# A transformer layer on one core: block tails ahead of leftovers, other places for group loads, maxima sent by ScalarE, scaling on GpSimd, and the readback of the sums one step later

## The chip, the cores and the metric

The kernel runs on one core of a Trainium2 chip. The time is the device time of one execution in microseconds. The core has five engines, each with an instruction queue of its own that it works off in order: TensorE (PE; matrix products, with PEld for the loading of the stationary operand), VectorE (DVE), ScalarE (ACT), GpSimd (POOL) and SyncE (SP). SP computes nothing; in this kernel it starts nearly all transfers between device memory and the core. A transfer waits on its issuing queue until what it reads is there and the buffer that it fills is free, and whatever stands behind it in that queue waits as well.

## The reference, cut to what matters

The input x is 16 batches of 512 rows by 512 columns, all in fp32. Each batch goes through attention and a gated feed-forward part:

```
n = layernorm(x)
q, k, v = n Wq + bq, n Wk + bk, n Wv + bv      # 32 heads of 16 columns
q, k = rope(q), rope(k)                        # y * cos + (halves swapped) * sin
out = softmax(causal(q k / 4)) v
x1 = x + layernorm(out Wo + bo)
h = silu((layernorm(x1) Wg) * gs) * ((layernorm(x1) Wu) * us)   # 1408 columns
x2 = x1 + layernorm((h Wd) * ds)
```

Wg, Wu and Wd hold only -1, 0 and 1 in the given data.

## The kernel before, in words

**Number format.** TensorE has a reduced fp32 format here (`fp32r`). Where an operand must stay exact it is cut into a high and a low part (`yh`, `yl`; `hh`, `hl`), and two products are summed. If the feed-forward weights survive the rounding to `fp32r` unchanged, they need only one part. The kernel tests this at run time: `check_weights` (L197) makes 22 checks, each a cast on ScalarE and a comparison on VectorE that counts differences, and a 23rd step, `total`, sums the counts into `flag`. After the front, `run` (L961) reads the flag on every engine and branches to one of two versions of the whole batch work. The data given here takes the first arm (`exact`).

**Staging.** `front` (L825) normalises and transposes batches 0 and 1, makes q, k and v of batch 0 and a part of v of batch 1, runs the weight checks and the first two groups of score maxima. `batches` (L983) then runs 16 batches of 8 groups (4 heads each) of 6 steps (`one_step`, L808). While batch b's attention is done step by step, TensorE is given a share of other work in each step from a list: the projections of batch b + 1, the output projection and the feed-forward part of batch b - 1, and the normalisation of batch b + 2. `run_list` (L712) cuts the list into shares of equal cost, one per step; items of cost 0 (loads, and the leftovers of blocks) fall where the list has them.

**A q or k block** (`qk_block`, L330) is four products into one of three PSUM banks and three things after it. `tail`: ScalarE writes the swapped halves with the bias (`ys`), VectorE writes `ya` = (product + bias) * cos, GpSimd multiplies `ys` by sin. `rest`: VectorE adds, ScalarE rounds to `yh`, GpSimd subtracts to `yl`. `store`: SP sends four pieces to device memory (`qd`, `kd`), from where `load_group` (L550) fetches them for a group of heads, the k rows doubled: 256 KB each for `q2`, `kh` and `kl`, three buffers each. In the front, `block` (L863) runs such a block; the `rest` and `store` of one block are kept in a list `then` and run after the second product of the next block.

**Scores.** In step i of group n, `scores` (L563) makes the transposed scores of group n for the weights (`st`, ScalarE's exponential, GpSimd's causal mask, all into `pt`), and the plain scores of a coming group (n + 1 in steps 0 and 1, n + 2 later), of which VectorE takes the maxima of every row (`s`, `nm`). When a group's maxima are complete, `turn_maxima` (L637) transposes them on TensorE (`pm`), splits them into `nmh` and `nml`, and SP puts them into the tile `mx` one step later; a short product then subtracts them from the transposed scores. The maxima of groups 0 and 1 are taken in the front; since they cross the branch, `keep_maxima` (L618) writes them to device memory (`mxd`) and `load_maxima` (L624) reads them after it.

**Values and sums.** `values` (L665) multiplies the weights with v (`av`), the columns' sums beside them. In step 0 of group n it finishes group n - 1 and copies the result to `ot`; SP stores it one step later (`od`). After the second group of a pair, `self.later` (which puts a call at the start of a later step) plans, for step 2, `sums` (L694): SP loads the sums and the values `oc`; for step 3, `sums_2` (L703): VectorE inverts, SP writes the reciprocals to device memory (`rd`) and reads them back, spread over 128 partitions, into a tile `rc` of the tag `xr`; for step 5: GpSimd multiplies `oc` by it.

**The tag xr.** A tag names a set of buffers that are used in turn; a new tile waits until one of them has been read for the last time. `xr` has two. The other users of it are the residual rows: `load_xr` (L394) loads 128 rows of x for the add after the output projection. `dense` (L498) loads the first two; `rest_1` of output block tb (`o_block`, L365) scales with ScalarE, adds the residual with GpSimd and then loads the rows of block tb + 2. Batches 1 to 13 have the same list, so the same pattern of steps.

The calls on an engine through `InOrder` (L39) keep program order on that engine; in the profile they all have line 49, so groups are told apart by the tiles' names.

Of the kernel before, what the change touches and what calls it, by code (L numbers as in the profile page):

```python
# [10 lines left out]
FP = mybir.dt.float32  # L11
FR = mybir.dt.float32r
AF = mybir.ActivationFunctionType
ALU = mybir.AluOpType
# [4 lines left out]
P = 128  # L19
# [34 lines left out]
class Block:  # L54
# [272 lines left out]
            tail,  # L327
        )

    def qk_block(self, b, name, c):  # L330

        bias = self.col["b" + name]
        st = {}

        def tail(p):
            ya = st["a"] = self.tile([P, T], "ya", bufs=1)
            ys = st["s"] = self.tile([P, T], "ys", bufs=1)
            for h in range(2):
                i, o = slice(64 * h, 64 * h + 64), slice(64 - 64 * h, 128 - 64 * h)
                self.act.activation(ys[o, :], p[i, :], AF.Identity, bias=bias[i, c : c + 1])  # L340
            self.dve.scalar_tensor_tensor(ya, p, bias[:, c : c + 1], self.cos, ALU.add, ALU.mult)
            self.pool.tensor_tensor(ys, ys, self.sin, ALU.mult)

        def rest():
            ya, ys = st["a"], st["s"]
            self.dve.tensor_tensor(ya, ya, ys, ALU.add)
            hi, lo = st["y"] = [self.tile([P, T], n, bufs=2, dtype=FR) for n in ("yh", "yl")]
            self.act.copy(hi, ya)
            self.pool.tensor_tensor(lo, ya, hi, ALU.subtract)

        def store():
            i = (b % 2) * NC + c
            for part, y in enumerate(st["y"]):
                if name == "q":
                    d = self.qd[i][:, part, :].rearrange("(h r) t -> h r t", r=DH)
                else:
                    d = self.kd[i][part].rearrange("(h r) t -> h r t", r=DH)
                for h in range(2):
                    self.sp.dma_start(out=d[:, 8 * h : 8 * h + 8, :], in_=y[64 * h : 64 * h + 64, :].bitcast(FP))

        return self.product(
            "p" + name, NC, lambda i: self.wts[b, name, c // 2][:, i, ts(c % 2, P)], lambda i: self.xnts["a", b][:, i, :], tail
        ), rest, store
# [254 lines left out]
    def keep_maxima(self, m):  # L618

        for i, t in enumerate(self.turned_maxima(m)):  # L620
            self.sp.dma_start(out=self.mxd[m][i].rearrange("j (b t) -> (j b) t", t=P), in_=t.bitcast(FP))
        del self.qs[m], self.ks[m]

    def load_maxima(self, m):  # L624
# [78 lines left out]
    def sums_2(self, b, c, s):  # L703
        i = (b % 2) * NC + c
        self.dve.reciprocal(s, s)
        self.sp.dma_start(out=self.rd[i].rearrange("h (u t) -> h u t", t=32), in_=s)
        rc = self.tile([P, T], "xr", bufs=2)
        self.sp.dma_start(out=rc, in_=self.rd[i].unsqueeze(1).to_broadcast([8, DH, T]))
        self.later(2, lambda: self.pool.tensor_tensor(self.ocs[b, c], self.ocs[b, c], rc, ALU.mult))


    def run_list(self, L, steps):  # L712
# [95 lines left out]
    def one_step(self, work, n, i):  # L808
        for f, args in self.todo.pop(self.step, []):
            f(*args)  # L810
        if i == 0 and n + 2 < self.B * NG:
            self.load_group(n + 2)
        m = n + 2 if i >= 2 else n + 1
        self.scores(n, None if m in self.mxs else m, i)
        if i == 2 and 0 <= n + 1 < self.B * NG and n + 1 not in self.mxs:
            self.turn_maxima(n + 1)
        next(work, None)
        if i == 3 and 0 <= n < self.B * NG:
            self.values(n, 0)
        if i == 0 and 0 <= n - 1 < self.B * NG:  # L820
            self.values(n - 1, 1)
            self.values(n - 1, 2)
        self.step += 1

    def front(self):  # L825

        nc = self.nc
        self.load_checks()
        checks = self.check_weights()

        def check(n):
            for _ in range(min(n, len(checks) - 1)):
                checks.pop(0)()

        def norm(b, tb):
            xt = self.xts.pop((b, tb))
            mr = self.stats(xt)

            def rest():
                xn = self.xns[("a", b), tb] = self.tile([P, C], "sg" if b and tb >= 2 else "xn", bufs=2)  # L840
                if b == 0:
                    self.dve.tensor_scalar(xn, xt, mr[0], mr[1], ALU.mult, ALU.add)
                else:
                    self.scaled(xn, xt, mr)

            return rest

        def turn(b, tb):
            for _, f in self.turn(self.xns, ("a", b), tb, self.xnts, ("xnta", "xntf")[b]):
                f()  # L850

        rest = None
        for tb in range(NB):
            now = norm(0, tb)
            if tb:
                rest()
                turn(0, tb - 1)
            rest = now
        rest()
        turn(0, NB - 1)  # L860
        then = []

        def block(name, c, n=0, scores=()):  # L863

            qk = name in "qk"
            items, *left = self.qk_block(0, name, c) if qk else (self.v_block(*c),)
            for k, (_, f) in enumerate(items):
                f()
                if k == 1:
                    for f in then:  # L870
                        f()
                    then.clear()
            then.extend(left)
            for m, i in scores:
                self.scores(-2, m, i)
            check(n)

        now = [norm(1, tb) for tb in range(2)]
        then += now
        block("q", 0, 2)  # L880
        then += [norm(1, tb) for tb in range(2, NB)]
        block("k", 0, 2)
        for tb in range(2):
            turn(1, tb)
        block("q", 1, 2)
        for tb in range(2, NB):
            turn(1, tb)
        self.load_w(0, "v", 0)
        block("k", 1, 2)
        self.load_w(0, "v", 1)  # L890
        self.sp.dma_start(out=self.xn1, in_=self.xnts["a", 1])
        block("q", 2, 2)
        block("v", (0, 0), 2)
        block("k", 2, 2)
        then += [lambda m=m: self.load_group(m) for m in range(2)]
        block("v", (0, 1), 2)
        block("q", 3, 1, [(0, 0), (0, 1)])
        block("v", (0, 2), 2, [(0, 2), (0, 3)])
        block("k", 3, 1, [(0, 4), (0, 5)])
        then += [lambda: check(len(checks)), lambda: self.keep_maxima(0)]  # L900
        block("v", (0, 3))
        nc.vector.tensor_scalar_mul(self.gh, self.col["gs"], 0.5)
        nc.vector.tensor_tensor(self.gu, self.gh, self.col["us"], ALU.mult)
        self.wts[1, "v", 0], self.wts[1, "v", 1] = self.wts[0, "v", 0], self.wts[0, "v", 1]
        i = 0
        for tb in range(2):
            for k, (_, f) in enumerate(self.v_block(1, tb)):
                f()
                if tb == 0 and k == 0:
                    checks.pop(0)()  # L910
                elif i < STEPS:
                    self.scores(-2, 1, i)
                    i += 1
        self.keep_maxima(1)
# [67 lines left out]

    def batches(self):  # L983
        B = self.B
        work = self.run_list(self.first_list(), NG * STEPS)
        for m in range(2):
            self.load_group(m)
            self.load_maxima(m)
        for b in range(B):
            if b:  # L990
                if b < B - 1:
                    L = self.dense(b)
                    L += self.gate_ups(b - 1, b + 2 if b + 2 < B else None, b + 2 == B)
                    if b < B - 2:
                        L += self.downs(b - 1, b + 2)
                else:
                    down = [self.downs(b - 2, None, tbs, True, True) for tbs in ((0, 1), (2, 3))]
                    L = down[0] + self.dense(b, down[1]) + self.gate_ups(b - 1, None, True)
                work = self.run_list(L, NG * STEPS)
            for g in range(NG):  # L1000
                for i in range(STEPS):
                    self.one_step(work, b * NG + g, i)
        L = [(0, lambda half=half: self.load_w(B - 1, "o", half)) for half in range(2)]
        work = self.run_list(L + self.downs(B - 2, None, (0, 1), True, True), STEPS + 2)
        for i in range(STEPS + 2):
            self.one_step(work, B * NG + i // STEPS, i % STEPS)
        for _, f in self.laid(self.last_list()):
            f()
# [61 lines left out]
```

## Time and profile before

| | us |
|---|---|
| median of 3 runs | 3239.6 (3237.93 to 3242.63) |
| profiled execution | 3243.39 |
| its span, first to last instruction | 3241.7 |
| PE busy | 3109.2 (96% of the span) |
| DVE, ACT, POOL busy | 1888.3, 1542.5, 1384.1 |
| DMA, mean over the span | 146 GB/s |

The profile is one execution. Busy time counts computing instructions alone; the start of a transfer appears on the queue that issues it (SPq), its end as the releaser of what waits for it. A row of a timeline gives the start, the duration, the engine, the operation with output and inputs by tile, and in brackets how long the engine stood idle before it and what ended that. The granted clock of PE is 1.00 at full speed and 0.5 at half. The first 115 us of the span are the front, the branch follows at 115 us, and the batches take about 192 us each.

### The profile page before, as it was taken

How to read it: one execution, taken by the hardware profiler on the slowest of the kernel's cores; microseconds unless marked ns; L12 is line 12 of the kernel's file. 1: busy time of each engine (PE TensorE's matmuls, PEld its weight loads, DVE VectorE, ACT ScalarE, POOL GpSimd, SP SyncE). 2: the span in 40 equal slices, each digit the busy share in tenths (PEclk: the TensorE clock that was granted, in tenths of full speed). 3: DMA queues.
4: the chain of work that ended last, by engine and by line, in shares of the span. 5: the costliest groups of instructions: out<-in, count | busy, mean ns of one | idle time of the engine just before them, and what ended most of it. 6: DMA issues, size and time to landing. Idle time of an engine off the chain costs nothing.

```text
span 3241.7 us, 59284 instructions
## 1 busy us (share of the span) xinstructions
PE 3109.2 (96%) x21258; PEld 1746.0 (54%) x21258; DVE 1888.3 (58%) x5911; ACT 1542.5 (48%) x2243; POOL 1384.1 (43%) x1933
## 2 busy tenths in 40 slices
PE   6789999999999999999999999999999999999988
PEld 2234564645546465564646556464555646555556
DVE  4355656656566565656656565665657556575633
ACT  4244545445454445545445454544545454553432
POOL 3033544344454435445343454534445442543443
PEclk8689999999999999999999999999999999999999
DMA  7254534535344453534435253453525345343422
GB/s 259 100 189 148 178 128 142 174 121 185 103 165 138 150 171 115 189 100 162 156 125 194 99 182 121 152 167 126 193 94 167 133 153 166 124 156 109 133 99 70
DMA packets 228385, 473.02 MB, mean 146 GB/s; under 512 B 41136, under 2 KB 45232, under 8 KB 227648
## 3 DMA queue, kind: packets, MB, share of 16 engines
q1 hardware_dynamic: 227648, 468.08, 42.9%
q8 instruction: 170, 2.79, 0.3%
q14 instruction: 135, 1.11, 0.1%
q10 hardware_dynamic: 432, 1.05, 0.1%
HBM read 347.39 MB, written 125.34 MB: 146 GB/s over the span
## 4 chain that ended last, share of the span: by engine, by line
PE 85%; DMA 4%; DVE 3%; ACT 2%; issue 1%; POOL 1%; SPq 1%; ACTq 0%; DVEq 0%; POOLq 0%
PE st L49 16%; PE pu L49 11%; PE pg L49 10%; PE av L49 9%; PE pd L49 9%; PE po L49 7%; PE pq L49 7%; PE pv L49 6%; PE pk L49 6%; PE s L49 3%; DMA kl<-kd 2%; PE px L49 1%; SPq L49 1%; DVE s L49 1%; ACT pt L49 1%
## 5 line engine op out<-in xcount | busy, mean ns | idle before, releaser
L49 DVE CUSTOM_DVE_ANT_0 s<-s,mask 128x128 f32<-128x128 f32 (+1 forms) x2032 | 973.7, 510 | 739.1 <-PE s L49 550.8
L49 ACT ACTIVATE pt<-st 128x1024 f32<-128x1024 f32 (+1 forms) x768 | 677.0, 881 | 780.8 <-PE st L49 764.4
L49 POOL TENSOR_SCALAR_AFFINE_SELECT pt<-pt 128x256 f32<-128x256 f32 (+1 forms) x768 | 394.0, 513 | 1209.0 <-ACT pt L49 1200.0
L49 PEld LDWEIGHTS st<-q,kh 32*128 32x128 f32 x2048 | 191.9, 184 | 467.2 <-issue 235.6
L49 PE MATMUL st<-q,kh 32*128 32x512 f32 (+3 forms) x2048 | 411.8, 399 | 19.7 <-ACT pt L49 13.3
L49 PE MATMUL s<-kh,q 32*128 32x128 f32 (+1 forms) x2032 | 410.6, 399 | 18.1 <-DMA kh<-kd 11.4
L49 PE MATMUL s<-kl,q 32*128 32x128 f32 (+1 forms) x2032 | 340.3, 322 | 13.1 <-DMA kl<-kd 13.0
L49 PE MATMUL st<-mx,one 2*128 2x512 f32 (+3 forms) x2048 | 334.1, 322 | 4.7 <-DMA mx<-nml 4.6
L49 PE MATMUL st<-q,kl 32*128 32x512 f32 (+3 forms) x2048 | 333.8, 322 | 0.1
L49 PE MATMUL av<-pt,v 128*32 128x512 f32 (+3 forms) x4096 | 333.8, 444 | 0.0
L49 POOL TENSOR_TENSOR hl<-ht,hh 128x512 fp32r<-128x512 f32 (+1 forms) x192 | 229.6, 1196 | 183.9 <-ACT hh L49 176.3
L49 PE MATMUL pd<-wd,hl 128*128 128x512 f32 x704 | 289.0, 411 | 10.8 <-POOL hl L49 10.8
L49 PE MATMUL pd<-wd,hh 128*128 128x512 f32 x704 | 290.8, 413 | 2.2 <-ACT hh L49 2.2
L49 DVE DVE_READ_ACCUMULATOR2_ANT nm<- 128x1 f32 x2048 | 289.9, 142 | 0.0
L49 PE MATMUL pg<-xntf,wf 128*128 128x512 f32 x704 | 287.0, 408 | 1.5 <-ACT xntf L49 1.5
L49 PE MATMUL pu<-xntfl,wf 128*128 128x512 f32 x704 | 284.0, 403 | 0.0
L49 PE MATMUL pu<-xntf,wf 128*128 128x512 f32 x704 | 283.5, 403 | 0.0
L49 PE MATMUL pg<-xntfl,wf 128*128 128x512 f32 x704 | 281.1, 399 | 0.6 <-DVE xntfl L49 0.6
L49 PE MATMUL pv<-w,xnta 128*128 128x512 f32 x464 | 235.4, 640 | 12.7 <-DMA w<-in_wv 12.7
L49 PE MATMUL po<-w,oc 128*128 128x512 f32 x512 | 244.5, 610 | 2.5 <-DMA w<-in_wo 2.5
L49 PE MATMUL pq<-xnta,w 128*128 128x512 f32 x480 | 237.7, 625 | 8.8 <-DVE ya L49 6.6
L49 PE MATMUL pk<-xnta,w 128*128 128x512 f32 x480 | 237.3, 611 | 3.2 <-DVE ya L49 2.6
(118 smaller groups left out, 4969.0 us busy)
## 6 DMA issues: line engine op xcount, KB each, us to landing
wf<-wgs SPq DMA_DIRECT2D x176, 512.0 KB
q<-qd SPq DMA_DIRECT2D x130, 256.0 KB
kh<-kd SPq DMA_DIRECT2D x130, 256.0 KB
kl<-kd SPq DMA_DIRECT2D x130, 256.0 KB
od<-ot SPq DMA_DIRECT2D x128, 256.0 KB
w<-in_wo SPq DMA_DIRECT2D x34, 512.0 KB
xr<-in_x SPq DMA_DIRECT2D x66, 256.0 KB
w<-in_wq SPq DMA_DIRECT2D x32, 512.0 KB
```

The source lines that it names most:

```text
L49: return self.tc.keep_in_program_order(f(*args, **kwargs))
```

## The change

- `qk_block` has a parameter `spare`: where it is true, `ya` and `ys` are tiles of the tag `y` (two buffers) instead of `ya` and `ys` (one each). The front sets it for k blocks.
- In the front, `block` runs all products of a block with its tail first, and then the leftovers of the block before.
- The scaling of batch 1's rows in the front is done by GpSimd instead of ScalarE.
- The order of blocks, checks, transposes, weight loads and score steps in the front is another one. Group 0's operands are loaded ahead of the last but one k block, group 1's after the last v block of batch 0; before, both were loaded in the v block after the last but one k block. The first scores stand after the second v block. The weight check's sum comes one product later, the maxima of group 0 are kept after it.
- `keep_maxima` issues its transfers on ScalarE's queue instead of SP's.
- After the branch, group 0 and its maxima are loaded, then the first share of the work list is run ahead of step 0 (49 shares instead of 48). Group 1 is loaded in step 0 behind group 2, its maxima in step 2. The two conditions on the group number in `one_step` are written for this.
- `sums_2` only writes the reciprocals; the new `sums_3`, one step later, reads them back, and the product stays in step 5.

```diff
--- before.py
+++ after.py
@@ -327,14 +327,15 @@
             tail,
         )
 
-    def qk_block(self, b, name, c):
+    def qk_block(self, b, name, c, spare=False):
 
         bias = self.col["b" + name]
         st = {}
 
         def tail(p):
-            ya = st["a"] = self.tile([P, T], "ya", bufs=1)
-            ys = st["s"] = self.tile([P, T], "ys", bufs=1)
+
+            ya = st["a"] = self.tile([P, T], "y" if spare else "ya", bufs=2 if spare else 1)
+            ys = st["s"] = self.tile([P, T], "y" if spare else "ys", bufs=2 if spare else 1)
             for h in range(2):
                 i, o = slice(64 * h, 64 * h + 64), slice(64 - 64 * h, 128 - 64 * h)
                 self.act.activation(ys[o, :], p[i, :], AF.Identity, bias=bias[i, c : c + 1])
@@ -618,7 +619,7 @@
     def keep_maxima(self, m):
 
         for i, t in enumerate(self.turned_maxima(m)):
-            self.sp.dma_start(out=self.mxd[m][i].rearrange("j (b t) -> (j b) t", t=P), in_=t.bitcast(FP))
+            self.act.dma_start(out=self.mxd[m][i].rearrange("j (b t) -> (j b) t", t=P), in_=t.bitcast(FP))
         del self.qs[m], self.ks[m]
 
     def load_maxima(self, m):
@@ -704,9 +705,12 @@
         i = (b % 2) * NC + c
         self.dve.reciprocal(s, s)
         self.sp.dma_start(out=self.rd[i].rearrange("h (u t) -> h u t", t=32), in_=s)
+        self.later(1, self.sums_3, b, c)
+
+    def sums_3(self, b, c):
         rc = self.tile([P, T], "xr", bufs=2)
-        self.sp.dma_start(out=rc, in_=self.rd[i].unsqueeze(1).to_broadcast([8, DH, T]))
-        self.later(2, lambda: self.pool.tensor_tensor(self.ocs[b, c], self.ocs[b, c], rc, ALU.mult))
+        self.sp.dma_start(out=rc, in_=self.rd[(b % 2) * NC + c].unsqueeze(1).to_broadcast([8, DH, T]))
+        self.later(1, lambda: self.pool.tensor_tensor(self.ocs[b, c], self.ocs[b, c], rc, ALU.mult))
 
 
     def run_list(self, L, steps):
@@ -810,9 +814,12 @@
             f(*args)
         if i == 0 and n + 2 < self.B * NG:
             self.load_group(n + 2)
+            if n == 0:
+                self.load_group(1)
+                self.later(2, self.load_maxima, 1)
         m = n + 2 if i >= 2 else n + 1
-        self.scores(n, None if m in self.mxs else m, i)
-        if i == 2 and 0 <= n + 1 < self.B * NG and n + 1 not in self.mxs:
+        self.scores(n, None if m < 2 else m, i)
+        if i == 2 and 0 <= n + 1 < self.B * NG and n > 0:
             self.turn_maxima(n + 1)
         next(work, None)
         if i == 3 and 0 <= n < self.B * NG:
@@ -838,10 +845,7 @@
 
             def rest():
                 xn = self.xns[("a", b), tb] = self.tile([P, C], "sg" if b and tb >= 2 else "xn", bufs=2)
-                if b == 0:
-                    self.dve.tensor_scalar(xn, xt, mr[0], mr[1], ALU.mult, ALU.add)
-                else:
-                    self.scaled(xn, xt, mr)
+                (self.pool if b else self.dve).tensor_scalar(xn, xt, mr[0], mr[1], ALU.mult, ALU.add)
 
             return rest
 
@@ -863,42 +867,41 @@
         def block(name, c, n=0, scores=()):
 
             qk = name in "qk"
-            items, *left = self.qk_block(0, name, c) if qk else (self.v_block(*c),)
-            for k, (_, f) in enumerate(items):
+            items, *left = self.qk_block(0, name, c, name == "k") if qk else (self.v_block(*c),)
+            for _, f in items:
                 f()
-                if k == 1:
-                    for f in then:
-                        f()
-                    then.clear()
-            then.extend(left)
+            for f in then:
+                f()
+            then[:] = left
             for m, i in scores:
                 self.scores(-2, m, i)
             check(n)
 
         now = [norm(1, tb) for tb in range(2)]
         then += now
-        block("q", 0, 2)
-        then += [norm(1, tb) for tb in range(2, NB)]
+        block("q", 0, 1)
         block("k", 0, 2)
+        now = [norm(1, tb) for tb in range(2, NB)]
         for tb in range(2):
             turn(1, tb)
+        then += now
         block("q", 1, 2)
+        self.load_w(0, "v", 0)
+        block("k", 1, 2)
         for tb in range(2, NB):
             turn(1, tb)
-        self.load_w(0, "v", 0)
-        block("k", 1, 2)
         self.load_w(0, "v", 1)
         self.sp.dma_start(out=self.xn1, in_=self.xnts["a", 1])
         block("q", 2, 2)
         block("v", (0, 0), 2)
+        self.load_group(0)
         block("k", 2, 2)
-        then += [lambda m=m: self.load_group(m) for m in range(2)]
-        block("v", (0, 1), 2)
-        block("q", 3, 1, [(0, 0), (0, 1)])
-        block("v", (0, 2), 2, [(0, 2), (0, 3)])
-        block("k", 3, 1, [(0, 4), (0, 5)])
-        then += [lambda: check(len(checks)), lambda: self.keep_maxima(0)]
-        block("v", (0, 3))
+        block("v", (0, 1), 2, [(0, 0), (0, 1)])
+        block("q", 3, 1, [(0, 2)])
+        block("v", (0, 2), 2, [(0, 3)])
+        block("k", 3, 2, [(0, 4)])
+        block("v", (0, 3), len(checks), [(0, 5)])
+        self.load_group(1)
         nc.vector.tensor_scalar_mul(self.gh, self.col["gs"], 0.5)
         nc.vector.tensor_tensor(self.gu, self.gh, self.col["us"], ALU.mult)
         self.wts[1, "v", 0], self.wts[1, "v", 1] = self.wts[0, "v", 0], self.wts[0, "v", 1]
@@ -906,9 +909,13 @@
         for tb in range(2):
             for k, (_, f) in enumerate(self.v_block(1, tb)):
                 f()
-                if tb == 0 and k == 0:
+                if tb == 0 and k == 1:
+                    for f in then:
+                        f()
                     checks.pop(0)()
-                elif i < STEPS:
+                if tb == 0 and k == 2:
+                    self.keep_maxima(0)
+                if tb or k >= 2:
                     self.scores(-2, 1, i)
                     i += 1
         self.keep_maxima(1)
@@ -982,10 +989,10 @@
 
     def batches(self):
         B = self.B
-        work = self.run_list(self.first_list(), NG * STEPS)
-        for m in range(2):
-            self.load_group(m)
-            self.load_maxima(m)
+        work = self.run_list(self.first_list(), NG * STEPS + 1)
+        self.load_group(0)
+        self.load_maxima(0)
+        next(work)
         for b in range(B):
             if b:
                 if b < B - 1:
```

## The prediction

> **What bounds the kernel now.** I read the busy shares first (PE 3109.2 of 3241.7 us), then a table of stretches (columns: length, busy us and count of PE, PEld, DVE, ACT, POOL, granted clock, DMA share, GB/s):
>
> ```profile
> core 0: us, PE busy (x) PEld busy (x) DVE busy (x) ACT busy (x) POOL busy (x), PEclk, DMA share, GB/s
> 64.00:71.00 7.00, 0.01 (x2) 0.04 (x2) 3.13 (x5) 4.43 (x6) 2.13 (x2) 0.76 0.63 200
> 95.00:115.00 20.00, 19.30 (x49) 7.12 (x49) 8.92 (x34) 1.32 (x3) 0.00 (x0) 0.58 0.02 5
> 115.00:133.00 18.00, 2.64 (x7) 1.41 (x8) 0.10 (x1) 1.02 (x1) 0.41 (x1) 0.61 0.71 250
> 133.00:150.00 17.00, 17.00 (x74) 6.66 (x72) 4.58 (x20) 4.25 (x5) 2.09 (x4) 0.51 0.00 1
> 300.00:2800.00 2500.00, 2468.82 (x17284) 1398.89 (x17284) 1513.99 (x4768) 1240.00 (x1809) 1118.67 (x1561) 1.00 0.44 147
> ```
>
> From 300 to 2800 us TensorE sets the time: 31 us idle in 2500. Anything that stalls PE there is lost for good, and little can be won. The front and the branch (to 150 us) hold what can be won: PE idles, and behind each idle stretch it runs at half clock (95 to 112 and 133 to 149.5 us, a pv pair 2.05 us instead of 1.05). Next I asked who crosses the branch when:
>
> ```profile
> L965 POOLq COMPARE_BRANCH  x1: 40/40/40, 96.3 to 96.3; - x1
> L965 PEldq COMPARE_BRANCH  x1: 90/90/90, 114.7 to 114.7; - x1
> L965 SPq COMPARE_BRANCH  x1: 49/49/49, 115.6 to 115.6; - x1
> ```
>
> GpSimd crossed 18 us before PE: the branch is no barrier. SP came last because it still had to send the second maxima (ready at 114.8).
>
> Last I took the stretch of the steady batches in which the change moves a load. SP's timeline (start, duration):
>
> ```profile
> 1115.68 0.34 SPq L49 DMA_DIRECT2D xr<-in_x  x1
> ...
> 1119.07 0.45 SPq L49 DMA_DIRECT2D rd<-sum  x1
> 1122.68 0.59 SPq L49 DMA_DIRECT2D xr<-rd  x1
> 1123.36 0.59 SPq L49 DMA_DIRECT2D mx<-nmh  x1
> 1124.01 0.57 SPq L49 DMA_DIRECT2D mx<-nml  x1
> 1127.39 0.33 SPq L49 DMA_DIRECT2D xr<-in_x  x1
> ```
>
> and GpSimd's, with one row from 230 us (in brackets: idle before it, and what ended that), and PE's wait behind it:
>
> ```profile
> 230.04 1.26 POOL L49 TENSOR_TENSOR oc<-oc,xr 128x512 f32<-128x512 f32 x1 [5.23 <-DMA xr<-rd]
> ...
> 1126.10 1.27 POOL L49 TENSOR_TENSOR x<-x,xr 128x512 f32<-128x512 f32 x1
> 1127.32 1.28 POOL L49 TENSOR_TENSOR oc<-oc,xr 128x512 f32<-128x512 f32 x1
> 1128.56 0.41 POOL L49 TENSOR_SCALAR_AFFINE_SELECT pt<-pt 128x256 f32<-128x256 f32 x1
> ...
> 1130.15 1.28 POOL L49 TENSOR_TENSOR x<-x,xr 128x512 f32<-128x512 f32 x1 [0.30 <-DMA xr<-in_x]
> ```
>
> ```profile
> 1137.58 0.28 PE L49 MATMUL pm<-ident,nm 128*16 128x128 f32 x1 [0.45 <-DVE ya L49]
> ```
>
> To be seen: the tag xr has two buffers. The last residual load (1127.39) left the moment the third residual add ended (1127.37), whose buffer it takes; the readback of the sums (1122.68) had taken the other one.
>
> **What the Trainium skill says.** TensorE: Matmul & The Clock Gate, HAM oscillation: PE gaps of a few microseconds cost again as half clock. The trace agrees; it even stays cold for 17 us at work. DMA: Bandwidth & Descriptors, "Issuing engines are not separate DMA queues": an issue from ScalarE saves sequencer time only. So the maxima move no sooner; SP is merely free. GPSIMD Engine Reference, 3.1: 769 ns for 512 elements of a tight one-input loop, the nearest price for the moved scaling.
>
> **Front, part by part** (times of the profiled execution).
> *Tail ahead of leftovers, scaling on GpSimd.* Two stalls: q1's first product waits until 32.76 for the tail of k0, which stood behind two 0.75 us scalings and a cast on ACT. After: k0 ends at 25.3, ys on ACT to 26.7, ya on DVE to 27.5, so q1 starts at 27.5: 5.2 us sooner. Price of a scaling on GpSimd, not in the trace: between 0.64 (its 128x512 affine select) and 1.27 (two-input row); I take 0.9. Four of them, each pair queued behind a ys product (1.28): the first pair lies beside k0, the second ends at 38.8 us, so the transposes and q2 wait from 34.7 to 39.4. The k blocks' ya and ys take the tag y, idle in the front, so a k tail needn't wait for q's leftovers; that costs nothing. wv's second half is sent behind q1's store at 43 and lands near 46.5 (before: 46.46 and 51.66), so v waits some 2 us more. q2 ended at 48 before, now near 45.
> *Group loads.* Group 0's load follows q2's store: q2's yl at about 52, four stores of 0.6 us, kl issued at 54.5 and 4.8 us to land (as 67.59 to 72.4): scores from 59 us instead of 72.4, with q3 not yet done (3.6 us): 8 to 10 us ahead. From there DVE is the limit: maxima 8.5, nine checks of 1.26 (11.3), ya and adds 3.5: 23.3 us, so the last check ends at about 83, against 94.5. Group 1's load now stands behind k3's store (yl at 82): kl lands at about 87, so PE waits some 5 us for the checks and 2 for kl, and runs cold. Remaining: 5 pv pairs of 2.05 and scores of 6.2 at half clock, 16.5 us: front's end at 102 instead of 114.4. **Gain 12** (5 to 18).
> *Maxima by ScalarE.* Two issues of 0.4 us on ACT, which waits 0.8 us for nml before the second; behind it only v copies. SP's last work in the front is group 1's load, so it crosses at about 86 and loads group 0, maxima, xnta and wv (2.8 MB at 250 GB/s: 11 us) under the end of the front. PE's waits of 5.2 (kh) and 10.8 us (w) go: **gain 16**. If the branch held SP back, the group and weights would still come some 5 us sooner for two groups fewer ahead. PE then goes through the first steps warm: half of the 17 us at 0.51 clock, **gain 8** (0 to 8.5).
> *First batch.* 49 shares instead of 48 put the wq load one step earlier relative to PE but still behind the same od store, so its wait at 157.5 grows from 1.5 to 4 us: loss 2.4. Groups 1 and 2 are loaded at step 0 and maxima 1 at step 2, needed at steps 6, 2 and 6; SP is far ahead by then, so this costs nothing (if SP weren't, some 3 us per group). The new tests on the group number name the same groups. At 226 us SP waits 5.2 us for rd and PE 4.6 for mx behind it; mx now goes ahead, but the product's 5.23 us wait on GpSimd stays: gain 0 to 5, I take 2.4. Sum of the front: **36** (22 to 48).
>
> **The readback a step later.** In three of a batch's four cases nothing happens: SP waits for rd to land anyhow (1.4 to 2.5 us), and the two maxima, 1.3 us, fit into this. In the fourth the readback passes the last residual load in SP's order. In program order: rd, maxima, xr (this takes the first free buffer at once, that of the second add, 1121.34), then the readback, which must have the buffer of the third add: issue at 1127.4 instead of 1122.68. It takes 3.65 us or more to land (226.19 to 230.04: 3.85; others 3.63 to 3.72 where GpSimd waited). The product stands in GpSimd's queue right behind that add: it starts at 1131.1 instead of 1127.32, **3.8 us later**. Behind it:
> - the mask (1128.56) is late: PE's last av products wait 1.15 us (1131.7 to 1132.85);
> - the last residual add comes 3.5 us later (its own 0.3 wait goes); DVE's statistics stood ready for it at 1131.4, and DVE takes in order: i=1 maxima, ya sum, then ACT's yh and ys, DVE's ya, then pm on PE. In this chain PE already waits 0.45 us, so there is no slack: pm at 1141.05 instead of 1137.58.
> That is 3.45 us of PE per batch, in batches 1 to 13 (the last add's wait of 0.2 to 0.4 us for xr stands 13 times; in 14 and 15 the third add is over before rd lands): 45 us. A gap of 2.5 us may cost a half-clock window too: waits of 1.0 to 1.8 us at the batch ends did so four times in a dozen (3.4 us, half of it lost). At two in five of 13: 9 us. **Loss 54** (40 to 67).
>
> Sum: 3243.4 (span 3241.7 and 1.7 around it) - 36 + 54 = 3261.4; the median lies 3.8 below the profiled execution, so **3257.6**.
>
> **Rivals.**
> 1. *Front gain stands, the readback costs little (faster).* If DVE and PE find other work for the 3.8 us, a third of it passes on: 13 x 1.2 = 16; 3239.6 - 36 + 16 = 3220; with none, 3204. It decides below 2.8 us of PE per batch (36/13). For: GpSimd is busy only 45% of the steady stretch. Against: POOL is busy 14.9 of 19 us at 1119 to 1138, and PE waits at the end of just this chain.
> 2. *Balance (same).* Front 45, no clock loss: 3239.6.
> 3. *Branch holds SP or wv lands late:* front only 20, 3274; against it GpSimd's crossing at 96.3.
> 4. *The change doesn't do what it says:* the readback was never what PE waited for in the steady part: no row of PE's waits there names rd, so there is nothing to gain from it.
>
> **How the numbers follow.** Main case 0.62 (own range 3246 to 3274), rival 1 0.20, balance 0.13, rival 3 or more clock loss 0.05. Within 0.2% (6.5 us, about what a measurement can tell) lies the balance: same 0.13, faster 0.20, slower 0.67. Range 3212 to 3280: it leaves out half of rival 1 and the far end.
>
> **What would show it.** Right: SP crossing well before PE, no wait for w in the branch, the front's end near 102; steady batches of 195 us instead of 191.5 (first residual add to the next batch's); thirteen waits of 3.5 us for xr<-rd on GpSimd, and pm waiting some 2.5 us. Wrong: batches still of 191.5 us, or the readback ahead of the last residual load on SP. The front is wrong if the checks on DVE end near 95 as before.

## The result and the profile after

The changed kernel takes 3288.6 us (median of 4 runs, 3286.0 to 3295.0), the kernel before 3241.1 on the same chip (with a fourth run beside the three of the table above, whose median was 3239.6): ratio 1.015, 95% interval 1.0131 to 1.0168. It is 47.5 us slower, where 18 us were predicted (3257.6, with 3280 as the upper end). The direction was right, the size was not.

The profiled execution took 3285.98 us (span 3284.2). First the table of stretches of the kernel after (length, busy us and count of PE, PEld, DVE, ACT, POOL, granted clock, DMA share, GB/s), with the edges moved to where its front and branch now lie:

```profile
64.00:71.00 7.00, 6.93 (x27) 3.16 (x28) 6.65 (x17) 4.92 (x6) 2.34 (x2) 1.00 0.41 147
90.00:113.00 23.00, 17.20 (x44) 6.53 (x43) 9.16 (x34) 1.68 (x4) 0.00 (x0) 0.50 0.32 109
113.00:125.00 12.00, 10.99 (x39) 4.67 (x39) 0.36 (x2) 2.05 (x2) 0.82 (x2) 0.51 0.49 185
300.00:2800.00 2500.00, 2437.19 (x16906) 1377.85 (x16901) 1486.51 (x4672) 1211.63 (x1769) 1091.83 (x1524) 0.99 0.44 145
```

The hole at 64 us is gone, and the wait of 10.8 us for `w` at the branch has shrunk to 5.1. But PE runs at half clock from 87 us, the end of its wait for the checks' sum, to 125 us. In the long steady stretch PE idles 63 us where it idled 31, with 378 matmuls fewer done in the same 2500 us. Next, who crosses the branch when (the times are the first and the last of two crossings; the first counts here):

```profile
L972 SPq COMPARE_BRANCH  x2: 41/47/53, 89.3 to 3279.9; - x2
L972 PEldq COMPARE_BRANCH  x2: 90/1963/3836, 109.1 to 3273.0; - x2
```

SP is 20 us ahead of PE, as forecast. Now the steady batch, the same place as in the profile before (the first residual add is at 1116.93 here, 1114.39 there). SP, then GpSimd, then PE:

```profile
1121.62 0.45 SPq L49 DMA_DIRECT2D rd<-sum  x1
...
1123.91 0.34 SPq L49 DMA_DIRECT2D xr<-in_x  x1
1129.93 0.62 SPq L49 DMA_DIRECT2D xr<-rd  x1
```

```profile
1128.63 1.27 POOL L49 TENSOR_TENSOR x<-x,xr 128x512 f32<-128x512 f32 x1
1133.87 1.26 POOL L49 TENSOR_TENSOR oc<-oc,xr 128x512 f32<-128x512 f32 x1 [3.97 <-DMA xr<-rd]
1135.09 0.41 POOL L49 TENSOR_SCALAR_AFFINE_SELECT pt<-pt 128x256 f32<-128x256 f32 x1
...
1136.34 1.28 POOL L49 TENSOR_TENSOR x<-x,xr 128x512 f32<-128x512 f32 x1
```

```profile
1135.55 0.63 PE L49 MATMUL av<-pt,v 128*32 128x256 f32 x4 [1.06 <-POOL pt L49]
...
1143.59 0.28 PE L49 MATMUL pm<-ident,nm 128*16 128x128 f32 x1 [2.25 <-DVE ya L49]
```

The whole chain is there. The last residual load has gone ahead of the readback and taken the free buffer; the readback leaves at 1129.93, 0.03 us after the third residual add (1128.63 + 1.27) gives its buffer up, 8.3 us behind `rd` instead of 3.6; GpSimd stands still for 3.97 us; the mask and the last residual add behind it are late; PE waits 1.06 us for the mask and 2.25 us, instead of 0.45, for `ya`, an operand that is late because the last residual add is. This happens in 13 batches: from 300 to 3150 us PE waits 25.8 us in 13 pieces for `ya` before `pm` (before: 6.0 in 13) and 14.5 us in 13 pieces for the mask (before: none).

Against the kernel before, the first residual add of the first batch comes 14.9 us sooner (329.3 against 344.2), the one 13 batches on 40.8 us later (2888.3 against 2847.5). So of 36 us of expected gain in the front 15 are there in this execution, and the batches lose 55.7. Two questions for experiments: is it really the readback, and by which link; and where did the gain of the front go?

### The profile page after: what moved, and what is told of

Its sections match the earlier page's. It is cut to its first block, busy times and chain, and to the rows that moved or that the text cites. A ratio compares the mean times of both kernels' runs of the same rounds, so it can differ in the third digit from the quotient of the medians.

```text
span 3284.2 us, 59251 instructions
## 1 busy us (share of the span) xinstructions
PE 3132.9 (95%) x21258; PEld 1754.2 (53%) x21258; DVE 1891.6 (58%) x5911; ACT 1538.2 (47%) x2239; POOL 1387.5 (42%) x1937
## 5 line engine op out<-in xcount | busy, mean ns | idle before, releaser
L49 PE MATMUL av<-pt,v 128*32 128x512 f32 (+3 forms) x4096 | 342.7, 444 | 15.6 <-POOL pt L49 15.6
L49 PE MATMUL pk<-xnta,w 128*128 128x512 f32 x480 | 254.1, 649 | 1.7 <-DVE ya L49 1.1
```

Source lines behind the costliest of these rows:

```text
L49: return self.tc.keep_in_program_order(f(*args, **kwargs))
```

## The experiments

All runs carry out the whole computation. Ratios are to the kernel before on the same chip, whose median was between 3243.9 and 3244.8 us. e1 to e4 ran on one chip and e5 to e10 on another, so the later ones are compared with e4 by their ratios.

### Is it the readback, and by which link?

**e1: the whole change without the later readback.** In `sums_2`:

```diff
-        self.later(1, self.sums_3, b, c)
+        rc = self.tile([P, T], "xr", bufs=2)
+        self.sp.dma_start(out=rc, in_=self.rd[i].unsqueeze(1).to_broadcast([8, DH, T]))
+        self.later(2, lambda: self.pool.tensor_tensor(self.ocs[b, c], self.ocs[b, c], rc, ALU.mult))
```

> The whole change, with the readback back in the step of the reciprocals. Theory (the readback a step later is what costs): the loss of the steady batches, 59 us from the first residual add to the end, goes, and the front keeps its 15: 3241 - 15 = 3226 us (3220 to 3232). GpSimd's thirteen waits of 3.65 to 4.4 us for xr<-rd go, PE's thirteen waits for ya come back from 2.3 to 0.5 us each. Rival (the new front or GpSimd's scaling brings the loss, by the clock or the order of the queues): the time stays above 3260 us.

Measured: 3235.9 us, ratio 0.9972 (0.9961 to 0.9982). The thirteen waits are gone (PE's waits for `ya`: 6.1 us in 13), and the batches take the time that they took before (2499.8 us over the same 13 batches; before 2503.4). The theory holds on the batches, but its 3226 us is missed by 10: the front's part is worth 9 us (6 to 13), less than the 15 in the profile of the changed kernel.

**e2: the later readback alone**, `sums_2` and `sums_3` of the change in the kernel before.

> The kernel before, with the later readback alone. Theory: the whole steady loss and no gain of the front: 3241 + 59 = 3300 us (3290 to 3308), with thirteen waits of 3.65 us or more on GpSimd. Rival (loss only together with the new front): below 3270 us.

Measured: 3299.4 us, ratio 1.0164 (1.0143 to 1.0186), so 53 us (46 to 60) for this edit alone, with the same waits (27.7 us for `ya`, 17.1 for the mask, 13 pieces each). The two parts add up: -9 and +53 make 44, the whole change measured 47.5 with an interval of 42 to 54. So nothing shows that the rest of the change takes part in the loss. In e2's profile the 13 batches take 48.1 us longer than before; the first residual add comes 1.5 us sooner, and the stretch behind the 13 batches takes 7.1 us longer, of which 5 is lost clock.

**e3: the later readback in another buffer**, in the first pair of groups of a batch, which is the case that waits.

```diff
-        rc = self.tile([P, T], "xr", bufs=2)
+        rc = self.tile([P, T], "y" if c == 0 and b < self.B - 2 else "xr", bufs=2)
```

> The whole change, the readback still a step later, but in the fourth case of each batch (and only there) its tile takes a buffer of the tag y, so that it needn't wait for the third residual add. Theory (the shared buffer is the wait): the readback leaves some 4.5 us sooner, the thirteen waits on GpSimd fall below 1 us, and the time is 3226 to 3235 us. Rival (the later step itself, or the readback's place behind the last residual load in SP's order, is what costs): 3275 us or more.

Measured: 3234.0 us, ratio 0.997 (0.9956 to 0.9985). SP's timeline in the same batch:

```profile
1101.21 0.34 SPq L49 DMA_DIRECT2D xr<-in_x  x1
1102.63 0.61 SPq L49 DMA_DIRECT2D y<-rd  x1
```

The readback still stands behind the maxima and behind the last residual load, and now leaves 3.7 us behind `rd` (1098.89). GpSimd's product starts right after the third add (1107.15, no wait). So neither the step nor the place in SP's order cost anything; the shared buffer did.

**e4: the product one step later as well**, the readback as late as in the changed kernel.

```diff
-        self.later(1, lambda: self.pool.tensor_tensor(self.ocs[b, c], self.ocs[b, c], rc, ALU.mult))
+        self.later(2, lambda: self.pool.tensor_tensor(self.ocs[b, c], self.ocs[b, c], rc, ALU.mult))
```

> The whole change, and the product of sums and values one step later too, so that nothing on GpSimd stands behind it for 3.8 us; the readback is as late as in the changed kernel. Theory (the loss passes through GpSimd's queue: the mask and the last residual add behind the product): the thirteen waits go and most of the 59 us with them: 3228 to 3245 us. Rival (the late buffer and SP's order cost by themselves, since the last residual load and what stands behind it on SP come later): above 3270 us.

Measured: 3229.0 us, ratio 0.9945 (0.9927 to 0.9962). GpSimd in the same batch, where `rd` leaves at 1107.88 and the readback at 1116.20:

```profile
1118.26 1.27 POOL L49 TENSOR_TENSOR x<-x,xr 128x512 f32<-128x512 f32 x1
1120.74 1.28 POOL L49 TENSOR_TENSOR oc<-oc,xr 128x512 f32<-128x512 f32 x1
```

The readback is just as late as in the changed kernel (8.3 us behind `rd`), and nothing is lost: the last residual add now stands ahead of the product, and the product finds its operand landed. The late buffer costs only because the product on GpSimd waits for it in front of the mask and the last residual add. e4 also lies 7 us below e1 and 5 below e3, with four runs; its interval just touches e1's and overlaps e3's, so whether the later product gains something of its own isn't shown.

### Where did the front's gain go?

In the changed kernel SP crosses at 89.3 us and should send `wv` at once. It doesn't. SP, and its only wait between 94 and 112 us:

```profile
93.10 1.28 SPq L49 DMA_DIRECT2D mx<-mxd  x2
94.43 0.43 SPq L49 DMA_DIRECT2D xnta<-xn  x1
110.57 0.82 SPq L49 DMA_DIRECT2D w<-in_wv  x2
```

```profile
SPq L49 <- DMA mxd<-nmh: 15.7, 1, 15.7
```

`wv` waits for the write of group 1's maxima, though it neither reads nor overwrites anything of it. ScalarE starts this write only at 109.2 us:

```profile
109.21 0.31 ACTq L49 DMA_DIRECT2D mxd<-nmh  x1
```

So `wv` stands still for a transfer that has not even begun; a limit on the transfers in flight wouldn't explain that. Counted in program order, the first of `wv`'s two transfers is the eighth transfer behind this write (`nml`, `q`, `kh`, `kl`, two for `mx`, `xnta`, then `wv`). The guess: transfers of SP and ScalarE share eight completion counters in turn, so that each waits for the one eight places ahead, whoever issued it. e5 and e6 test it on e4.

**e5: group 1's maxima sent by GpSimd's queue.**

```diff
-            self.act.dma_start(out=self.mxd[m][i].rearrange("j (b t) -> (j b) t", t=P), in_=t.bitcast(FP))
+            (self.pool if m else self.act).dma_start(out=self.mxd[m][i].rearrange("j (b t) -> (j b) t", t=P), in_=t.bitcast(FP))
```

> The kernel of e4, and group 1's maxima written to device memory by GpSimd's queue instead of ScalarE's. In e4 SP sends wv only when that write has landed (15.4 us of wait on mxd<-nmh), though wv needs nothing of it. Theory (the wait belongs to ScalarE's transfers: SP's eighth transfer after one of them must wait until it has landed): SP sends wv before 97 us, PE's 5.1 us wait for w at the branch goes, the first residual add comes 5 us or more sooner than in e4 (333.7), the time falls by 5 to 12 us. Rival (wv waits for its buffer, or for the maxima whatever queue sends them): wv still leaves at 108 us or later and the time stays within 4 us of e4.

**e6: the first share of the list ahead of the load of the maxima.**

```diff
-        self.load_maxima(0)
         next(work)
+        self.load_maxima(0)
```

> The kernel of e4, with the first share of the list (xn of batch 1, wv) ahead of the load of group 0's maxima, so that this load and not wv is the eighth transfer behind ScalarE's write. Theory (place in the order of transfers): wv leaves SP at about 94 us and PE's 5.1 us wait for w goes; the load of the maxima now takes the wait until about 108.5 us and still lands before PE wants it, or costs PE at most 2 us at st; 4 to 12 us less than e4. Rival (wv waits for its buffer): wv still leaves at 108 us and the time stays within 4 us of e4.

Measured: e5 3229.1 us (0.9947; 0.9928 to 0.9965), e6 3228.6 us (0.9939; 0.9915 to 0.9964). SP in e5, then in e6:

```profile
95.15 0.38 SPq L49 DMA_DIRECT2D xnta<-xn  x1
95.59 0.90 SPq L49 DMA_DIRECT2D w<-in_wv  x2
```

```profile
93.67 1.65 SPq L49 DMA_DIRECT2D w<-in_wv  x2
111.23 1.20 SPq L49 DMA_DIRECT2D mx<-mxd  x2
```

In both `wv` goes out early. In e6 the wait has moved to the transfer that now has the eighth place: `mx`, the load of group 0's maxima, which in the changed kernel went out at 93 us. The theory holds on the place in the order, and the rival (`wv` waits for its buffer) is ruled out. PE's first product after the branch now follows the front's last `pm` by 0.95 us in both (5.5 us in e4). But of the 4 to 12 us expected in the time nothing is to be seen: both lie within 0.5 us of e4 by the medians and 2 by the ratios, as the rival had it, with intervals of 6 to 8 us on either side. The first residual add comes at 330.5 and 327.0 us against 333.7, 3.2 and 6.7 us sooner. This can't decide it: counted from the front's last `pm`, that add follows after 217 to 230 us in four executions with nearly the same work (the changed kernel, e1, e3, e4). So whether PE's wait of 5 us was worth 5 us of time stays open.

**e7: in e6, the products for v of batch 1 ahead of group 1's scores and of the checks' sum**, since PE's wait for that sum (in the changed kernel 4.06 us, ended at 87.71; in e6 the same length) is where the half clock begins.

```diff
-                    checks.pop(0)()
-                if tb == 0 and k == 2:
+                if tb == 1 and k == 0:
                     self.keep_maxima(0)
-                if tb or k >= 2:
-                    self.scores(-2, 1, i)
-                    i += 1
+        checks.pop(0)()
+        for i in range(STEPS):
+            self.scores(-2, 1, i)
         self.keep_maxima(1)
```

> The kernel of e6, and at the end of the front all products for v of batch 1 ahead of group 1's scores and of the sum of the checks, so that PE has 6 us of products where it waited 4.1 us for the sum. Theory (this wait of 4 us is what makes PE run at half clock from 87 to 125 us and so took most of the predicted gain of the front): PE runs the v products at full clock, the front's last pm comes at 98 to 102 us instead of 106.4, and the time is 6 to 14 us below e6. Rival (VectorE's checks and maxima set the end of the front whatever PE's clock is, or PE falls to half clock anyway while it waits for group 1's operands): last pm at 104 us or later, and less than 4 us below e6.

Measured: 3222.0 us, ratio 0.9924 (0.9896 to 0.9952), 6.6 us below e6, with overlapping intervals. PE at the end of its front:

```profile
87.77 0.19 PE L49 MATMUL pm<-ones,odd_sum 128*1 128x1 f32 x2
89.82 0.50 PE L49 MATMUL s<-kh,q 32*128 32x512 f32 x2 [1.86 <-DMA kh<-kd]
...
99.48 0.38 PE L49 MATMUL pm<-ident,nm 128*16 128x128 f32 x1 [1.11 <-DVE nm L49]
100.33 2.05 PE L49 MATMUL pv<-w,xnta 128*128 128x512 f32 x2 [0.46 <-DMA w<-in_wv]
```

The products run at full clock in the former hole and the front ends at 99.5 us, 9.7 sooner than in e6. The theory holds for that. The rival is right on the rest: after the wait for group 1's operands PE is at half clock from 91.8 us on all the same (the pair at 100.33 takes 2.05 us), and stays there until about 120. This is the lowest median of the study, 22 us below the kernel before.

**e8 to e10: one part of the front undone in e4.**

```diff
e8:
-            self.act.dma_start(out=self.mxd[m][i].rearrange("j (b t) -> (j b) t", t=P), in_=t.bitcast(FP))
+            self.sp.dma_start(out=self.mxd[m][i].rearrange("j (b t) -> (j b) t", t=P), in_=t.bitcast(FP))
e9:
-                (self.pool if b else self.dve).tensor_scalar(xn, xt, mr[0], mr[1], ALU.mult, ALU.add)
+                if b == 0:
+                    self.dve.tensor_scalar(xn, xt, mr[0], mr[1], ALU.mult, ALU.add)
+                else:
+                    self.scaled(xn, xt, mr)
e10:
-            for _, f in items:
+            for k, (_, f) in enumerate(items):
                 f()
-            for f in then:
-                f()
-            then[:] = left
+                if k == 1:
+                    for f in then:
+                        f()
+                    then.clear()
+            then.extend(left)
```

> The kernel of e4, with the maxima written to device memory by SP's queue again. Theory (SP's freedom from these two writes is what lets it cross the branch early, and this is the greatest part of the front's gain): SP loads group 0 and wv only behind the last write, after 108 us, PE's first product after the branch comes at 121 to 126 us instead of 111.9, and the time is 8 to 14 us above e4, so about that of the kernel before. Rival (the time won at the branch is lost again later in the first batch, by half clock or by the waits for wq, kh and mx): less than 4 us above e4.

> The kernel of e4, with batch 1's rows scaled by ScalarE again. Theory (with the tails ahead of the leftovers, it matters little which engine scales: the second pair waited on GpSimd behind two other operations, and PE 4.7 us for it): PE's wait for sg is 2 to 5 us, the last pm of the front stays within 1.5 us, the time within 4 us of e4. Rival (the scalings delay ScalarE's tails as they did before): the first product of q1 2 us or more later than 28.6, the last pm 2 us or more later, and the time 4 us or more above e4.

> The kernel of e4, with a block's leftovers again run behind the second product of the next block, ahead of that block's tail. Theory (the front's gain begins here: the tails come sooner): q1's first product at 31 us or later instead of 28.6, the last pm 2 to 5 us later, the time 2 to 6 us above e4. Rival (VectorE's checks and maxima, which set the pace from 60 to 88 us, hide it): the last pm within 1.5 us and the time within 2 us of e4.

| | median, us | ratio (95%) | q1's first product | last pm of the front | first product behind the branch |
|---|---|---|---|---|---|
| e4 | 3229.0 | 0.9945 (0.9927 to 0.9962) | 27.5 | 106.4 | 111.9 |
| e8, SP sends | 3239.4 | 0.9988 (0.9979 to 0.9997) | 27.8 | 110.7 | 124.0 |
| e9, ScalarE scales | 3232.0 | 0.9961 (0.9946 to 0.9976) | 28.3 | 108.0 | 113.8 |
| e10, leftovers first | 3229.8 | 0.9961 (0.9951 to 0.9971) | 29.8 | 109.4 | 115.0 |

PE's row in e8, where SP sends `wv` at 115.65:

```profile
124.00 2.05 PE L49 MATMUL pv<-w,xnta 128*128 128x512 f32 x2 [12.96 <-DMA w<-in_wv]
```

e8 came out as its theory said: `wv` leaves behind the last write, PE waits 13 us, and the median is 10 us above e4's (14 by the ratios). The cleaner comparison is with e9 and e10 on the same chip: e8 lies 7 and 10 us above them (9 by the ratios), and its interval lies above both of theirs. Sending the maxima from ScalarE is most of what the front gained; all else that e4 changes, its way with the readback included, is worth 4 us together (1 to 7). e9's theory holds on the time, 3 us above e4 (5 by the ratios) and within the intervals. Its two moments were just missed: with ScalarE scaling PE waits 1.8 us for `sg` instead of 4.7 (2 to 5 expected), and the last `pm` comes 1.6 us later (at most 1.5 expected); PE also loses 4.0 us for `y` before q1 and q2. e10 missed on its first number (q1 at 29.8, 2.3 us later than in e4, but not at 31) and on the time, no different from e4's within the intervals; that the tails come sooner was worth nothing that these runs can tell. Its last `pm` is 3 us later than in e4, but among kernels with the same front as e4 that moment lies anywhere from 106.4 to 109.8 us, so it decides nothing.

## Why the prediction was right or wrong

**The readback: right in mechanism, and its sum close.** Predicted 54 us (40 to 67); the edit alone measures 53 (46 to 60). Link by link, predicted and in the batch shown: product late, GpSimd standing 3.8 and 3.97 us; wait for the mask 1.15 and 1.06; wait before `pm` some 2.5 and 2.25 (2.0 in the mean of the 13); thirteen batches and thirteen waits. Of the 48.1 us that e2's 13 batches take longer, 5.2 is lost clock (the sum over short stretches of their length times one minus the granted clock, less the 6.8 us of before). That leaves 3.3 us per batch, predicted 3.45. The term for half clock, 9 us, was the weak one: it is 5 in e2 and 17 in the profile of the changed kernel. That the sum agrees to 1 us is partly luck, since e2 also holds the small gain at `mx` (below) and the 7.1 us behind the 13 batches, which nothing ties to the readback. Rival 4 (the change doesn't do what it says, since no wait of PE named `rd`) was right too on its half: the change removed no wait in batches 1 to 13. Rival 1 (the delay is absorbed) falls with e2: 3.3 us per batch, where it needed less than 2.8. Rival 2 (balance) needed a front of 45 us.

**The front: wrong, 36 us predicted, 9 measured** (e1; 6 to 13), below the lower bound of 22. This is the step that failed. Three of its terms fell short: the front's end came later than the sum of its links said, a load that needs nothing of the front's end could not leave at once, and PE came cold to the branch. By its terms:

- *Front's end, gain 12.* The end came at 108.5 us, predicted 102: gain 5.6. The first links were well priced: q1 at 28.6 us (27.5), a scaling on GpSimd 0.98 us in the first pair (0.9; in the second pair 1.24), the transposes at 40.5 (39.4), 2.06 us for the second half of `wv` (2). Then the first scores started at 63.5 us, not 59: q2 ended three microseconds later than assumed, and its add on VectorE stood behind two checks, so its `yl` came at 56 us and not 52. This lateness was passed on: VectorE's work from there to the last check took 23.9 us (23.3), and PE got group 1's operands at 90.7 us (about 87). What PE still had to do then took 17.8 us (16.5). The sum had a slip too: 87 and 16.5 make 103.5, not 102.
- *Branch, gain 16.* SP crossed as predicted (89.3; predicted 86), but the prediction took it that a load that needs nothing of the front's end can leave. The wait on ScalarE's write held `wv` for 15.7 us, and PE still waited 5.1 us: gain 10.9. Rival 3 named a late `wv`, without a reason for it, and set the front at 20; e5 and e6 show the reason, the place in the order of transfers. That the missing 5.1 us of idle time are 5.1 us of the kernel's time isn't shown (e5, e6).
- *Warm clock, gain 8.* The prediction held that PE, no longer idle at the branch, would start warm. But PE was cold before: it fell to half clock in the 4.06 us wait for the checks' sum, in the front. Four kernels with the same order of work up to 165 us (the changed kernel, e1, e3, e4) have a mean granted clock of 0.85, 0.81, 0.86 and 0.82 from 0 to 300 us; the kernel before has 0.83. In their mean nothing was gained, and what one execution happens to get moves it by some 7 us either way (0.81 to 0.86 of 300 us is 15 us). The 15 us of gain in the first profile are so best read as 9, the wait for `mx` of the next point and a lucky clock; the shares aren't shown.
- *wq later, loss 2.4:* PE's wait was 4.1 us, predicted 4. Right. *Mx ahead of rd, gain 2.4:* PE's wait of 4.6 us for `mx` is gone from the changed kernel and from e2, and still 4.2 in e1, without the later readback. Right in kind; in e2 the first residual add comes 1.5 us sooner.

The missed terms are 6.4, 5.1 and 8 us, together 19.5 of the 27 missing; the 2.4 of `mx` can't be in e1. Some 5 us aren't located; the interval of e1 alone is 7 us wide.

So the sum of +18 became +47.5 almost by the front alone. The range was too narrow because it let the front fall short by 14 us at most, as though its three gains could not fail together; two of them rested on one assumption, that PE comes busy to the branch and finds its operands there.

## What to carry to other kernels

When a transfer is moved in a queue, look at which buffer it will find free: a tag with two buffers shared by two users gives the buffer to whoever comes first in program order, and the late one waits for the other user's work. What such a delay costs is decided by what stands behind the waiting instruction on its engine: another buffer (e3) or a later place for the consumer (e4) both made 53 us vanish. And before counting on a load to leave early, count the transfers ahead of it: here one that waits for late data on another queue held back the eighth behind it, and moving one load in the order was enough to move the wait. What such a freed wait is worth has to be measured by itself: at the branch here it was too small to be seen.

## What was not expected of the hardware

- **A load waited for a write on another queue that it has nothing to do with.** `wv` (changed kernel, e4) or `mx` (e6), always the eighth transfer in program order behind ScalarE's write, left only when that write had landed, 15 to 16 us after the transfer ahead of it on SP; with the write on GpSimd's queue (e5) only the load that needs those maxima waited for it. Shared completion counters would explain this; the trace shows the waits, not the counters, and whether the chip or the compiled program sets them isn't shown.
- **Half clock at full work.** The Trainium skill's page TensorE: Matmul & The Clock Gate, Part 1, has the array warm again after some 3.4 us of sustained activity. The traces here don't agree. In the changed kernel it stays at half clock for 37 us, of which PE stands idle for some 5 in one piece, at the branch; PE is busy 11.0 of 12 us in 113 to 125. In e4 it is busy for all of the same 12 us at a clock of 0.50:

```profile
113.00:125.00 12.00, 12.00 (x44) 4.65 (x42) 1.85 (x8) 3.07 (x3) 1.46 (x3) 0.50 0.31 117
```

  From the first product behind the branch the half clock went on for 10 or 11 us (changed kernel, e3), 21 (e4) or 24 (e1) in the same order of work. What counts as activity here, and what lets the half clock end, stays open.
